# Four graph layers in a four-stage pipeline: layer 0 moved from the first stage to the second

## The chip, the cores and the metric

The kernel runs on one core of one Trainium2 chip. The metric is the device time of one execution in microseconds; the median of three runs before the change is 5727.59 us (5719.75 to 5731.36).

## What is computed

64 graphs, each with 256 nodes, 128 features a node and a symmetric 0/1 adjacency matrix, go through four graph layers. Each layer's result is added to its input and normalised over the features. Shortened:

```python
x: (64, 256, 128) f32, adj: (64, 256, 256) f32 of zeros and ones

# layer 0: maximum over neighbours
p = x @ (W1 - W2);  q = x @ W2
h = relu(p[:, :, None] + q[:, None] + b) * adj[..., None]
x = layernorm(x + max(h, axis=2))
# layer 1: two aggregations and an own term
in_rep, out_rep, node_rep = elu(x @ W.T + b) for three W, b
x = layernorm(x + tanh(concat(adj @ in_rep, node_rep, adj.T @ out_rep) @ W_upd.T + b_upd))
# layer 2: two normalised graph convolutions
x = layernorm(x + norm_A @ (elu(norm_A @ (elu(elu(x @ W0 + b0)) @ W1) + b1) @ W2) + b2)
# layer 3: a message for each edge, normalised, through gelu, summed over neighbours
msg = gelu(layernorm(m_j[:, None] + m_i[:, :, None] + b1))
x = layernorm(x + layernorm(concat(x, sum_j msg * adj) @ W2 + b2))
```

Layers 0 and 3 are the heavy ones: they have a vector of 128 features for each pair of nodes. About one pair in eight is an edge.

## The kernel before

**The sparse layout.** For each graph the nodes are sorted by degree, and the neighbours of all nodes are listed in slots: a node with many neighbours fills many slots. The slots of one half of the nodes lie in `WIDTH` = 4800 columns, and `hot` is a one-hot matrix in fp8 that says, for each column, which node is the neighbour. A matmul of features with `hot` thus gathers the neighbours' features: L665 does it for layer 0, with q split into three bf16 parts, and L728 for layer 3. Layer 0 goes over the 4800 columns of each half in ten tiles of up to 512. In each, three matmuls (L665) write a `bigp` buffer in PSUM, small matmuls (L681) with `lack` and `lack_t` push unfilled slots to a very low value, and `fold` (L492) takes the maximum into `lanes`. After ten tiles the result is transposed (L691), put back in the nodes' order by a matmul with `permT` (L699), added to x and normalised into x1 (L705 to L711). Layer 3 goes over the same columns in tiles of 1024, TODO = 10 of them: `sums_of` makes `pre` (L728, L732), its squares and their sums (L736, L743), and sends the variances through DRAM to get a scale for each column; `last` multiplies (L839), applies Gelu (L841) and folds the sums (L492).

**The stages.** Four generator functions hold the work of one graph. `first` loads the graph, makes the transposed adjacency `aT` (L516, L519), counts and ranks degrees with Sign (L528 to L551), makes the permutation `perm` (L556, L560) and its transpose `permT` (L566 to L581), ranks the neighbours (L585 to L591), writes `hot` (L629, L635), and then does layer 0 (from the projections of L647 to x1). `second` is layer 1 (L215 to L259). `third` is layer 2 (L261 to L317), the projections of layer 3 (L793 to L815) and the first four tiles of `sums_of`. `last` is the other six tiles, Gelu and the sums, and the update with the output.

**The order.** `steps` walks over 64 graphs. In one tick, `last` of graph g, `third` of g+1, `second` of g+2 and `first` of g+3 are recorded together. Each `yield` ends a piece of a stage. `together` takes the pieces in turn: it always calls the generator whose number of calls, divided by its weight, is lowest. The weights are written by hand:

```python
STAGES = [(last, 34), (third, 34), (second, 14), (first, 44)]
e = min(gens, key=lambda e: e[0] / e[1])
```

In this kernel they are the numbers of calls that each stage takes: 34, 34, 14 and 44. The recorded order is the priority order of a scheduler, which may put an instruction that it takes to be ready ahead of one that isn't. After that each engine runs its instructions in a fixed order.

**Buffers.** Pool `state` has two buffers for each name, `hold` has four (`permT`, `lack`, `hot`), `pair` and `work` have one. PSUM is parted in two: four `mm` buffers for all small products (`psum()`), and four `bigp` buffers that layer 0 and layer 3 share. All loads and stores are issued by SP.

Of the kernel before, what the change touches and what calls it, by code (L numbers as in the profile page):

```python
# [10 lines left out]
BF16 = mybir.dt.bfloat16  # L11
# [32 lines left out]
def kernel(  # L44
# [12 lines left out]
    H = N // P  # L57
# [64 lines left out]
    with tc.tile_pool(name="prep", bufs=1) as prep, tc.tile_pool(  # L122
        name="ps_prep", bufs=2, space=bass.MemoryType.PSUM
# [33 lines left out]
    class Shared:  # L157
# [5 lines left out]
        def psum(self):  # L163
            return self.ps_mm.tile([P, 512], F32, name="mm")
# [189 lines left out]
    def sparse(ctx):  # L354
# [24 lines left out]
        g_s0, g_n, g_w = RECTS[-1]  # L379

        ROWS = SLOTS + 2
# [68 lines left out]
        state = ctx.enter_context(tc.tile_pool(name="state", bufs=2))  # L450
        hold = ctx.enter_context(tc.tile_pool(name="hold", bufs=4))
        pair = ctx.enter_context(tc.tile_pool(name="pair", bufs=1))
        work = ctx.enter_context(tc.tile_pool(name="work", bufs=1))
        big = ctx.enter_context(tc.tile_pool(name="big", bufs=2))
        sh = Shared(work, state, ps_mm)
# [13 lines left out]
        def widen(ap, n):  # L469

            return ap.unsqueeze(1).broadcast_to([ap.shape[0], n, ap.shape[1]])
# [30 lines left out]
        def first(g, s):  # L502

            xn = sh.node_tile("x0")
            nc.sync.dma_start(xn, x[ds(g, 1)].rearrange("b (h p) d -> p (b h) d", p=P))
            an = state.tile([P, H, N], F32, name="an")
# [5 lines left out]
            aT = state.tile([P, H, N], F32, name="aT", bufs=3)  # L512
# [6 lines left out]
                nc.scalar.copy(aT[:, hj], pt[:, :N])  # L519
            nzT = as_bf16(aT)  # L520
            yield
            xT = sh.to_features(xn, "xT_0", 1)


            pd = psum()
# [31 lines left out]
            perm = state.tile([P, H, H, N], F32, name="perm", bufs=3)  # L557
# [14 lines left out]
            permT = hold.tile([P, H, H, N], F32, name="permT")  # L572
# [17 lines left out]
            lack = hold.tile([ROWS, H, N], BF16, name="lack")  # L590
# [15 lines left out]
                fl[:, 5:9].rearrange("p (a b) -> p a b", a=H), fv, -1.0, least, ALU.mult, ALU.add  # L606
            )
            nc.vector.tensor_max(viol, viol, fl)
            lack_t = pair.tile([ROWS, H, g_n, g_w], BF16, name="lack_t")
            for h in range(H):  # L610
                nc.vector.tensor_mul(lack_t[:, h], tail, widen(lack[:, h, :g_w], g_n))
            s.update(an=an, aT=aT, perm=perm, permT=permT, lack=lack)

            full = pair.tile([ROWS, H, N], BF16, name="full")
            nc.vector.tensor_scalar(full, lack, 0.0, None, ALU.is_equal)
# [9 lines left out]
            hot = hold.tile([P, H, WIDTH], FP8, name="hot")  # L625
# [8 lines left out]
            for h in range(H):  # L634
# [4 lines left out]
                    ALU.is_equal,  # L639
                    saturate=False,  # L640
                )
            yield
            s["hot"] = hot

            pq = psum()
            for h in range(H):
                nc.tensor.matmul(  # L647
# [129 lines left out]

        def second(g, s):

            yield from sh.layer_1(s, s["an"], s["aT"], s["x1"])  # L780

        def third(g, s):
# [94 lines left out]

        U = next(u for u in (UNROLL, 8, 4, 2, 1) if B % u == 0)
        STAGES = [(last, 34), (third, 34), (second, 14), (first, 44)]

        def steps(g0):
# [215 lines left out]
    with tc.tile_pool(name="flag", bufs=1) as fp, tc.tile_pool(  # L1097
        name="ps_flag", bufs=1, space=bass.MemoryType.PSUM
# [44 lines left out]
```

## Time and profile before

| | us |
|---|---|
| median of three runs | 5727.59 |
| the profiled execution | 5731.62 |
| its span | 5729.7 |
| PE, PEld busy | 4529.9, 2508.7 |
| DVE busy | 4834.4 |
| ACT busy | 4275.2 |
| ACT table loads of L841, L74, L194 | 686.4, 570.9, 283.5 |
| DMA, mean | 64 GB/s |
| granted TensorE clock, mean | 0.862 |

The span runs from the first to the last instruction. PE is the matmul engine, PEld its loading of weights, DVE the vector engine, ACT the scalar engine. By the chain that ended last, PE has 52% of the span, DVE 29%, ACT 11%, DMA 3%. The profile shows the same pattern for each graph from about the fourth on; it is best read one graph at a time.

### The profile page before, as it was taken

What the parts mean: (1) busy time and instruction counts of PE and PEld (TensorE: products, weight loads), DVE (VectorE), ACT (ScalarE), POOL (GpSimd) and SP (SyncE); (2) the same over time, 40 slices, a digit from 0 to 9 for tenths busy, and PEclk for the clock granted to TensorE, in tenths of its full rate; (3) what the DMA queues carried; (4) which work ended last, traced back from release to release, by engine and by line L of the source; (5) the groups of instructions that cost most, each with busy time, mean ns of one, the idle gap of its engine ahead of it and who ended that gap; (6) DMA issues with size and microseconds to landing.
All of it is one profiled execution on the core that took longest, in us unless ns stands there. A gap on an engine that the chain in (4) does not pass through costs nothing.

```text
span 5729.7 us, 83531 instructions
## 1 busy us (share of the span) xinstructions
PE 4529.9 (79%) x27408; PEld 2508.7 (44%) x27408; DVE 4834.4 (84%) x14654; ACT 4275.2 (75%) x6485; POOL 1.9 (0%) x10
## 2 busy tenths in 40 slices
PE   5878878878778778788788788787887887877875
PEld 2444444444444444444444444444444444444443
DVE  6788888888888888888888888888888888888876
ACT  2577777777777777777777777777777777777785
POOL 0000000000000000000000000000000000000000
PEclk8888889889889889888898898898888887888986
DMA  0122222222212221221221222122212212221222
GB/s 22 44 70 63 62 63 72 62 63 66 69 57 70 65 63 63 72 63 62 63 72 62 63 65 70 59 68 65 63 62 72 64 62 63 69 66 60 68 65 74
DMA packets 292813, 365.15 MB, mean 64 GB/s; under 512 B 151952, under 2 KB 210448, under 8 KB 292368
## 3 DMA queue, kind: packets, MB, share of 16 engines
q1 hardware_dynamic: 292368, 359.73, 20.0%
q8 instruction: 217, 3.56, 0.3%
q14 instruction: 228, 1.87, 0.1%
HBM read 345.07 MB, written 14.53 MB: 63 GB/s over the span
## 4 chain that ended last, share of the span: by engine, by line
PE 52%; DVE 29%; ACT 11%; issue 4%; DMA 3%; SPq 0%; DVEq 0%; POOL 0%; ACTq 0%
PE bigp L665 11%; PE bigp L728 8%; DVE pre L839 6%; PE mm L860 5%; DVE lanes L492 4%; PE mm L743 4%; DVE hot L629 4%; DVE pre L732 4%; DVE sums L492 3%; PE bigp L681 3%; DMA rs_s<-scale_line 2%; PE mm L870 2%; PE mm L296 2%; PE mm L699 2%; PE mm L647 2%
## 5 line engine op out<-in xcount | busy, mean ns | idle before, releaser
L665 PE MATMUL bigp<-hot,q 128*128 128x512 fp8e4 (+1 forms) x3840 | 1052.3, 371 | 66.6 <-DVE lanes L492 52.6
L728 PE MATMUL bigp<-hot,c 128*128 128x512 fp8e4 (+1 forms) x3840 | 928.8, 372 | 140.2 <-DVE pre L732 140.2
L732 DVE TENSOR_TENSOR pre<-bigp,dT 128x512 f32<-128x512 f32 (+6 forms) x1664 | 846.3, 530 | 37.8 <-PE bigp L728 33.5
L492 DVE TENSOR_TENSOR lanes<-bigp,lanes 128x512 f32<-128x512 f32 (+6 forms) x1536 | 772.7, 503 | 94.6 <-PE bigp L681 86.9
L839 DVE TENSOR_TENSOR pre<-pre,rs_s 128x1024 f32<-128x1024 f32 (+1 forms) x640 | 732.9, 1150 | 48.6 <-DMA rs_s<-scale_line 48.0
L736 ACT ACTIVATE sq<-pre 128x1024 f32<-128x1024 f32 (+1 forms) x640 | 638.5, 998 | 169.9 <-DVE pre L732 163.9
L841 ACT ACT_TABLE_LOAD x535 | 686.4, 1283 | 9.5
L492 DVE TENSOR_TENSOR sums<-pre,sums 128x1024 f32<-128x1024 f32 (+6 forms) x1024 | 628.8, 614 | 41.2 <-ACT pre L841 40.7
L745 ACT ACTIVATE row<-mm,eps_t 128x256 f32<-128x256 f32 (+1 forms) x640 | 289.6, 453 | 476.9 <-PE mm L743 476.7
L841 ACT ACTIVATE pre<-pre,be,g 128x1024 f32<-128x1024 f32 (+1 forms) x512 | 594.2, 1172 | 57.8 <-DVE pre L839 53.0
L743 PE MATMUL mm<-sq,ones 128*32 128x256 f32 (+1 forms) x5120 | 482.9, 440 | 135.2 <-ACT sq L736 135.2
L74 ACT ACT_TABLE_LOAD x445 | 570.9, 1283 | 7.5
L728 PEld LDWEIGHTS <-c 128*128 128x128 bf16 x3840 | 331.2, 98 | 550.5 <-issue 136.1
L665 PEld LDWEIGHTS <-q 128*128 128x128 bf16 x3840 | 310.8, 97 | 392.6 <-issue 112.0
L296 PE MATMUL mm<-aT,hs 128*128 128x256 f32 x512 | 232.3, 600 | 316.1 <-DVE hs L293 214.8
L629 DVE TENSOR_SCALAR hot<-rank 128x512 fp8e4<-128x512 bf16 (+5 forms) x1536 | 440.5, 348 | 0.0
L681 PEld LDWEIGHTS <-pick 42*128 42x128 bf16 x2944 | 155.8, 95 | 481.5 <-issue 474.2
L296 PEld LDWEIGHTS mm<-aT,hs 128*128 128x128 f32 x512 | 135.6, 293 | 425.8 <-issue 316.1
L860 PE MATMUL mm<-w3u,sums 128*128 128x128 f32 x2048 | 296.7, 289 | 18.4 <-DVE sums L492 16.1
L194 ACT ACT_TABLE_LOAD x221 | 283.5, 1283 | 3.9
L681 PE MATMUL bigp<-lack,pick 42*128 42x36 bf16 (+16 forms) x2944 | 285.7, 187 | 0.0
L860 PEld LDWEIGHTS mm<-w3u,sums 128*128 128x128 f32 x2048 | 254.5, 195 | 37.3 <-issue 17.6
(226 smaller groups left out, 7132.6 us busy)
## 6 DMA issues: line engine op xcount, KB each, us to landing
rs_s<-scale_line SPq DMA_DIRECT2D x512, 512.0 KB
rs_s<-scale_line SPq DMA_DIRECT2D x128, 352.0 KB
an<-in_adj SPq DMA_DIRECT2D x64, 256.0 KB
x<-in_x SPq DMA_DIRECT2D x64, 128.0 KB
line<-row SPq DMA_DIRECT2D x512, 4.0 KB
out<-o SPq DMA_DIRECT2D x64, 128.0 KB
fu<-fulls SPq DMA_DIRECT2D x192, 4.0 KB
vr<-line SPq DMA_DIRECT2D x192, 8.0 KB
```

The lines of the kernel that those rows point to most:

```text
L74: nc.scalar.activation(t, t, AF.Sqrt)
L492: nc.vector.tensor_tensor(lanes[:, :k, :w], src[:, i:i + k], lanes[:, :k, :w], op)
L629: nc.vector.tensor_scalar(hot[:, :, at:at + w], rank[:, :, :w], s0 + i + 1.0 - FAR, None, ALU.is_equal, saturate=False)
L665: nc.tensor.matmul(pt[:, :tl], q3[:, i, h], hot[:, h, t0:t0 + tl], start=i == 0, stop=False)
L681: nc.tensor.matmul(o_, l_, r_, start=False, stop=i == len(todo) - 1)
L728: nc.tensor.matmul(pt[:, :bl], c3[:, k, h], hot[:, h, t0 + b:t0 + b + bl], start=k == 0, stop=k == 2)
L732: nc.vector.tensor_add(block(pre[:, b:], n, w, at), block(pt, n, w, at), widen(dT[:, h, :w], n))
L736: nc.scalar.activation(sq[:, :tl], pre[:, :tl], AF.Square)
L743: nc.tensor.matmul(pr[q * Q:(q + 1) * Q, :tl // 4], ones[:, :Q], v4[:, :, q], start=True, stop=True)
L839: nc.vector.tensor_mul(pre[:, :tl], pre[:, :tl], rs[:, :tl])
L841: nc.scalar.activation(msg[:, :tl], pre[:, :tl], AF.Gelu, bias=be3, scale=g3)
L860: nc.tensor.matmul(pt[:, cols], lanes[:, k, cols], w3u[:, 1], start=k == 0, stop=False)
```

## The change

Layer 0 becomes a function of its own, `layer_0`, which `second` runs ahead of layer 1. With it goes the transpose of the node features, `xT_0`, which stood near the head of `first`. What layer 0 needs of `first` is handed on in `s`: `xn`, `hot`, `lack`, `lack_t` and `permT`. `lack_t` moves from the pool with one buffer to the one with two. The yield at the end of `hot` goes, one is put behind the transposes, and one between layer 0 and layer 1. The weights in `STAGES` stay as they are. The number of calls of `first` becomes 17, that of `second` 42.

```diff
@@ first
             yield
-            xT = sh.to_features(xn, "xT_0", 1)
 
             pd = psum()
...
-            lack_t = pair.tile([ROWS, H, g_n, g_w], BF16, name="lack_t")
+            lack_t = state.tile([ROWS, H, g_n, g_w], BF16, name="lack_t")
             for h in range(H):
                 nc.vector.tensor_mul(lack_t[:, h], tail, widen(lack[:, h, :g_w], g_n))
-            s.update(an=an, aT=aT, perm=perm, permT=permT, lack=lack)
+            s.update(xn=xn, an=an, aT=aT, perm=perm, permT=permT, lack=lack, lack_t=lack_t)
...
                     saturate=False,
                 )
-            yield
             s["hot"] = hot
 
+        def layer_0(s):
+
+            xn, hot, lack, lack_t, permT = (s[n] for n in ("xn", "hot", "lack", "lack_t", "permT"))
+            xT = sh.to_features(xn, "xT_0", 1)
+            yield
             pq = psum()
             for h in range(H):
...
@@ second
         def second(g, s):
 
+            yield from layer_0(s)
+            yield
             yield from sh.layer_1(s, s["an"], s["aT"], s["x1"])
```

More of the change, by code (lines that the diff above doesn't have):

```diff
@@ L641, in first @@
                 )
+            s["hot"] = hot
+        def layer_0(s):
+            xn, hot, lack, lack_t, permT = (s[n] for n in ("xn", "hot", "lack", "lack_t", "permT"))
+            xT = sh.to_features(xn, "xT_0", 1)
             yield
-            s["hot"] = hot
             pq = psum()
```

## The prediction

> **What bounds the kernel now.** Line numbers are those of the kernel before throughout. First the page: how full the engines are, and which waits the costly groups have.
>
> ```profile
> span 5729.7 us, 83531 instructions
> PE 4529.9 (79%) x27408; PEld 2508.7 (44%) x27408; DVE 4834.4 (84%) x14654; ACT 4275.2 (75%) x6485; POOL 1.9 (0%) x10
> L665 PE MATMUL bigp<-hot,q 128*128 128x512 fp8e4 (+1 forms) x3840 | 1052.3, 371 | 66.6 <-DVE lanes L492 52.6
> L629 DVE TENSOR_SCALAR hot<-rank 128x512 fp8e4<-128x512 bf16 (+5 forms) x1536 | 440.5, 348 | 0.0
> ```
>
> No engine is full; three lie between 75 and 84%, so the time is set by how the work of the four stages is laid side by side. The output transfers give the beat: the first is issued at 292.27, the 60th at 5441.70, so one graph takes (5441.70 - 292.27) / 59 = 87.28 us. Next, the busy time in the stretches of one such beat (columns: us, then PE, PEld, DVE, ACT, POOL busy, granted clock, DMA share, GB/s):
>
> ```profile
> 2566.00:2596.00 30.00, 18.64 (x99) 10.82 (x100) 22.84 (x73) 26.02 (x44) 0.00 (x0) 0.66 0.15 45
> 2596.00:2647.00 51.00, 49.04 (x324) 26.93 (x324) 46.52 (x140) 34.98 (x52) 0.00 (x0) 1.00 0.25 79
> 2566.00:2652.50 86.50, 70.57 (x433) 38.87 (x434) 74.86 (x229) 66.43 (x102) 0.00 (x0) 0.86 0.21 65
> 2652.50:2739.00 86.50, 69.93 (x427) 38.22 (x426) 75.29 (x228) 67.72 (x103) 0.00 (x0) 0.88 0.21 66
> ```
>
> The reader sees two regimes. For 30 us the small chained steps of `first`, layer 1 and layer 2 run, side by side: PE is busy 62%, DVE 76%. Then for 51 us layer 0's loop and the sums run: PE 96%, DVE 91%. One beat holds PE 70.2 and DVE 75.1 us of work. The view of waits says what the thin stretch waits for:
>
> ```profile
> PE mm L566 <- DVE perm L560: 245.5, 64, 5.1
> PE mm L296 <- DVE hs L293: 214.8, 67, 8.7
> DVE io L226 <- PE mm L223: 179.7, 64, 3.1
> PE mm L296 <- DVE vr L769: 101.3, 31, 8.7
> ```
>
> Per graph that is 3.8 us for the permutation, 4.9 for layer 2's first product and 2.8 for layer 1's. Last, single steps of the chain, by the timeline:
>
> ```profile
> 2569.59 0.69 PE L207 MATMUL mm<-ident,x 128*128 128x128 f32 x2
> 2642.37 0.38 PE L691 MATMUL mm<-ident,total_m 128*128 128x128 f32 x2
> 2642.59 1.95 PE L699 MATMUL mm<-mk,permT 128*128 128x128 f32 x16
> 2651.88 0.47 PE L207 MATMUL mm<-ident,x 128*128 128x128 f32 x1 [0.82 <-DVE x L180]
> 2572.30 0.76 DVE L226 TENSOR_TENSOR io<-mm,b_io 128x256 f32<-128x256 f32 x2 [3.11 <-PE mm L223]
> 2603.27 1.03 PE L240 MATMUL mm<-an,io 128*128 128x256 f32 x4
> 2580.82 1.28 ACT L194 ACT_TABLE_LOAD   x1
> ```
>
> Layer 0's tail, from L699's end (2644.54) to the transposes of x1 (2651.88), takes 7.3 us, and PE has 14 matmuls of L728 (3.5 us) to do in it. That is the cover to watch.
>
> **What the Trainium skill says.** "TensorE: Matmul & The Clock Gate" (the table of specifications) has the vector and scalar queues as strict FIFO, and lets the tensor queue only pull weight loads ahead; so an instruction that waits holds all behind it. The trace agrees: L566 waits 245.5 us with L743 and L296 behind it. The same page (Part 1) says that an idle tensor engine falls to half its clock: here 0.66 in the thin stretch, 1.00 in the dense one. "ScalarE: Activation LUTs" (What ACT_TABLE_LOAD costs) gives about 1283 ns for a switch of table; the trace has 1283. "Perfetto Trace Analysis" (Optimization Strategy) advises to interleave regimes with different limits; the change interleaves one pair and parts another.
>
> **The change part by part.** Per graph it moves, all from `first` to `second`: 2 transposes, 2 projections, 60 matmuls of L665 and 46 of L681, the folds, 4 transposes, 8 matmuls of L699 and a layernorm. None is added or dropped, no DMA is moved. Table loads in the built order go from 1301 to 1325 (0.4 a graph, 0.5 us on ACT, which has 20 us to spare a beat): nothing. `lack_t` gets a second buffer, and x0 is held one stage longer; its load for the next graph but one can start when L709 has read it, still a beat ahead: nothing. The chain of a graph keeps four stages.
>
> What counts is the order. `together` calls whichever generator has the lowest ratio of calls to weight. Before, calls and weights agree (34, 34, 14, 44). After, `first` has 17 calls under weight 44, and `second` 42 under 14. When `last` and `third` have made their 34, `second` has made 14; its other 28, half of layer 0 and all of layer 1, come with nobody beside them. The scheduler may still lift later ready work, but the built order of PE shows that it hardly does: L691, L699, L207, L223, L230, L238, L240, L249 stand in a row with no L665, L728 or L860 between. So layer 1 follows x1 at once, and layer 2 (L285) follows x2; before, both ran beside `first`.
>
> (1) The exposed chain S, from the last L691 to the next graph's first L665, each step from the rows of the timeline:
> - L691 to the end of L699: 2.2 (2642.37 to 2644.54).
> - to x1's transposes: 7.3 and 8.3 in two beats; I take 7, DVE having less beside it.
> - L207 to L226: 2.7 (2569.59 to 2572.30).
> - L226 0.7, Exp 0.6, one queued L839 1.2 of which 0.9 is seen, L200 and L201 1.1: 3.3.
> - L238 and L240 take 2.1, but ACT stands with load 1.28, Gelu 1.24, load 1.28, Exp 0.42 and copy 0.56 ahead of L249: 2.9 after L201.
> - L249's matmuls and two transposes: 2.2. L253, Tanh, L256: 1.5.
> - x2's layernorm: in DVE's order `kc` (L542) stands inside it and waits for L534, which waits for the aT copies, which ACT does after Tanh: 0.9 + 1.8; then four signs' worth of ACT, a load of 1.28, Sqrt, L75, L180: 6.5 together.
> - transposes, L285, q3: 3.0.
> Sum 31.3 us. PE work in it: 0.4 + 2.0 + 0.4 + 2.1 + 0.6 + 2.1 + 1.9 + 0.4 + 0.6 + 1.9 + 0.8 + 0.4 + 1.6 + 1.1 = 16.1. DVE work, read off its order: 68 instructions with 24.8 us of durations, less the 0.08 by which neighbours overlap (0.68 long, 0.60 apart), 19.3. So DVE idles 12 us in S alone, as much as it does now in a whole beat (87.3 - 75.1 = 12.2).
>
> (2) The rest M. Left are PE 70.2 - 16.1 = 54.1 and DVE 75.1 - 19.3 = 55.8. Now `first`'s chain (perm, rank, hot) lies beside layer 0 and layer 2, so its waits shrink: a gain. At the shares of the dense stretch M is 54.1 / 0.96 = 56.4 by PE and 55.8 / 0.91 = 61.3 by DVE. The 6.9 us of `hot` (440.5 / 64) need no PE, so DVE runs fuller there than 91%, up to 97%: 57.5. But while they run PE's four `bigp` buffers stand full (about 5 us), and it restarts at the lower clock. I take 60.
>
> Beat: 31.3 + 60 = 91.3, 4.0 more than 87.28. Over 59 beats 236 us. The ends: tick 0 loses layer 0, which ran alone (22 groups of L665 and L681 at 0.95, some 21 us); the tail, 282.2 us from the 60th output to the 64th, should keep its length within 5. Net -22. The profiled execution took 5731.62 around its span of 5729.7, so 5731.6 + 236 - 22 = 5946, and the median of the runs is 4 lower: 5942.
>
> Bounds: S from 27 (tail 5, no ACT hold, kc's wait hidden) to 35 (8.3 in the tail, each hop a little late); M from 57.5 to 63. Beat 84.5 to 98: 5545 to 6340.
>
> **The rivals.**
> - Covered, faster: layer 0's matmuls stand where PE now waits for perm and layer 2, 8.7 us a beat, and hot fills DVE's holes; S comes to 27.5, M to 57.5, the beat to 85.0: 5731 - 135 - 22 = 5574, and with DVE at 91% throughout (82.5) 5430. For it: those two waits are the largest of PE's. Against it: they pass to L207, L249 and L285, which now stand alone. It decides when S is below 28 with M below 59.
> - Heavier: every hop of S costs more than its bare row, and PE at half clock runs the start of M late; S 35, M 61, beat 96: 5731 + 515 - 20 = 6226. For it: the 0.66 clock, and 8.3 in one beat.
> - No change: gains and losses cancel, beat within 0.2 of 87.5: 5720.
> - That the change does nothing, the scheduler restoring the old order, the built order excludes.
>
> **How the numbers follow.** Likeliest, slower by the exposed chain: 0.48, 5942, its own range 5800 to 6080. Heavier 0.24. Covered 0.24. No change 0.04. A measurement of this kernel tells 0.2% (11 us) from no change. Faster 0.24, same 0.04, slower 0.72. The range goes to 5560 and 6300, leaving some 0.1 of each rival beyond.
>
> **What would show it.** Right: a beat near 91; PE waits for L180, L201 and L243 at L207, L238 and L249 of some 12 us a graph, with L566's wait below 1; a thin stretch of about 31 us with DVE near 60%. Wrong: DVE over 88% of the span, or layer 1's instructions found beside L665 in time. If the beat is longer but S is 31, M was mis-sized, and PE's waits for `pre` and `lanes` behind hot (L728, L665) will have grown.

## The result and the profile after

The changed kernel takes 6524.14 us, the median of four runs (6522.33 to 6529.15), beside 5729.48 us for the kernel before. The ratio is 1.139, with a 95% interval of 1.137 to 1.141: 13.9% slower, where 3.7% had been forecast. The profiled execution took 6522.96 us. All line numbers from here on are those of the changed kernel; from layer 0 on they lie some three to five above those of the kernel before (L665 is now L668, L691 is L694, L699 is L702, L728 is L731), and before it some one below (L560 and L566, of the permutation, are now L559 and L565).

The page of the changed kernel: span, busy time, and the group that waits longest.

```profile
span 6521.0 us, 83114 instructions
...
PE 4783.0 (73%) x27408; PEld 2664.2 (41%) x27408; DVE 4923.9 (76%) x14654; ACT 4322.3 (66%) x6509; POOL 1.9 (0%) x10
...
L207 PE MATMUL mm<-ident,x 128*128 128x128 f32 x512 | 185.2, 407 | 637.3 <-DVE x L180 637.3
```

PE runs the same 27408 matmuls, and is busy 253 us longer with them (4783.0 - 4529.9), at a mean granted clock of 0.838 where it was 0.862. It stands for another 538 us more (1738 against 1200). One line, the transposes of a normalised x, waits for 637 us.

The outputs give the beat: the first is issued at 277.21, the 60th at 6178.24, so a graph takes 5901.03 / 59 = 100.02 us, 12.74 more than before. The whole difference of the spans then adds up: 59 × 12.74 = 751.6, the head 15.1 shorter, the tail from the 60th output on 54.8 longer (342.8 against 288.0), together 791.3.

The stretches of one beat of the changed kernel, cut where layer 0 ends and where the next layer 0 begins (columns: us, then PE, PEld, DVE, ACT, POOL busy, granted clock, DMA share, GB/s):

```profile
2466.20:2500.10 33.90, 17.19 (x79) 11.88 (x78) 20.22 (x60) 24.80 (x43) 0.00 (x0) 0.69 0.15 48
2500.10:2565.19 65.09, 56.06 (x351) 28.80 (x350) 56.19 (x168) 43.07 (x60) 0.00 (x0) 0.92 0.20 62
2466.20:2565.19 98.99, 73.26 (x429) 40.68 (x428) 76.41 (x228) 67.87 (x103) 0.00 (x0) 0.84 0.18 57
```

The first line is the chain S of the prediction, the second its rest M. In S both PE (51%) and DVE (60%) are half idle. M is no longer like the dense stretch of before either: PE and DVE are busy 86% each, not 96 and 91%. Over 20 beats S is 34.3 us (32.7 to 35.5) and M 65.7.

What PE waits for in the changed kernel, from the view of waits (us in total, times, longest):

```profile
PE mm L207 <- DVE x L180: 637.3, 192, 10.7
PE mm L238 <- DVE io L201: 200.2, 64, 4.5
PE bigp L731 <- DVE pre L735: 177.3, 158, 2.8
...
PE mm L702 <- ACT mk L695: 79.6, 61, 1.4
...
PE mm L249 <- ACT ag L243: 43.2, 64, 0.7
...
PE mm L296 <- DVE hs L293: 12.5, 6, 3.3
...
PE mm L565 <- DVE perm L559: 5.7, 6, 4.6
```

The wait for the permutation has gone from 245.5 us to 5.7, and that of layer 2's product (L296) from 214.8 and 101.3 to 12.5. In their place stand L207, L238, L249 and L702, the steps of layer 0's tail and of layer 1, with next to nothing beside them. The waits of L207, L238 and L249 together are 13.8 us a graph ((637.3 + 200.2 + 43.2) / 64); some 12 had been named as the sign of this cause. PE's own timeline shows them one after the other (start, us, then what it is; in brackets the idle time before it and what ended that):

```profile
2468.86 1.16 PE L702 MATMUL mm<-mk,permT 128*128 128x128 f32 x8 [1.38 <-ACT mk L695]
2475.93 0.73 PE L207 MATMUL mm<-ident,x 128*128 128x128 f32 x2 [5.91 <-DVE x L180]
2477.12 2.07 PE L223 MATMUL mm<-w_ioT,xT 128*128 128x256 f32 x4 [0.46 <-ACT xT L209]
2482.91 2.04 PE L238 MATMUL mm<-aT,io 128*128 128x256 f32 x4 [2.86 <-DVE io L201]
2484.75 1.64 PE L240 MATMUL mm<-an,io 128*128 128x256 f32 x4
2487.07 0.49 PE L249 MATMUL mm<-w_updT,ag 128*128 128x128 f32 x2 [0.68 <-ACT ag L243]
...
2497.09 0.45 PE L207 MATMUL mm<-ident,x 128*128 128x128 f32 x1 [3.16 <-DVE x L180]
```

The order is the one that the prediction read off the built kernel: x1's transposes, layer 1, x2's transposes, each behind a wait. L240, which took 1.03 us where it stood in the dense stretch of before, takes 1.64 here.

### The profile page after: what moved, and what is told of

It reads as the page before. It is cut to its first block, busy times and chain, and to the rows that moved or that the text cites. A ratio compares the mean times of both kernels' runs of the same rounds, so it can differ in the third digit from the quotient of the medians.

```text
span 6521.0 us, 83114 instructions
## 1 busy us (share of the span) xinstructions
PE 4783.0 (73%) x27408; PEld 2664.2 (41%) x27408; DVE 4923.9 (76%) x14654; ACT 4322.3 (66%) x6509; POOL 1.9 (0%) x10
## 4 chain that ended last, share of the span: by engine, by line
PE 39%; DVE 30%; ACT 18%; DMA 9%; issue 4%; SPq 0%; DVEq 0%; ACTq 0%; POOL 0%
DVE pre L735 6%; PE bigp L731 5%; DVE hot L628 5%; DMA rs_s<-scale_line 5%; DVE lanes L492 4%; ACT L74 4%; PE mm L865 4%; PE mm L746 3%; PE bigp L668 3%; PE mm L815 3%; ACT pre L846 3%; ACT L846 3%; DVE sums L492 2%; DMA an<-in_adj 2%; PE mm L802 2%
## 5 line engine op out<-in xcount | busy, mean ns | idle before, releaser
L731 PE MATMUL bigp<-hot,c 128*128 128x512 fp8e4 (+1 forms) x3840 | 991.7, 378 | 211.4 <-DVE pre L735 177.3
L668 PE MATMUL bigp<-hot,q 128*128 128x512 fp8e4 (+1 forms) x3840 | 1045.7, 373 | 126.1 <-DVE lanes L492 71.5
L207 PE MATMUL mm<-ident,x 128*128 128x128 f32 x512 | 185.2, 407 | 637.3 <-DVE x L180 637.3
L492 DVE TENSOR_TENSOR sums<-pre,sums 128x1024 f32<-128x1024 f32 (+6 forms) x1024 | 628.5, 614 | 15.1 <-ACT pre L846 13.5
L748 ACT ACTIVATE row<-mm,eps_t 128x256 f32<-128x256 f32 (+1 forms) x640 | 289.4, 452 | 398.9 <-PE mm L746 398.2
L746 PE MATMUL mm<-sq,ones 128*32 128x256 f32 (+1 forms) x5120 | 460.4, 407 | 106.6 <-ACT sq L739 106.6
L731 PEld LDWEIGHTS <-c 128*128 128x128 bf16 x3840 | 345.9, 100 | 463.9 <-issue 179.7
L668 PEld LDWEIGHTS <-q 128*128 128x128 bf16 x3840 | 327.4, 98 | 426.5 <-issue 122.8
L207 PEld LDWEIGHTS mm<-ident,x 128*128 128x128 f32 x512 | 91.8, 180 | 724.7 <-DVE x L180 476.6
L865 PE MATMUL mm<-w3u,sums 128*128 128x128 f32 x2048 | 296.3, 289 | 16.1 <-DVE sums L492 16.1
L870 ACT COPY ak<-mm 128x256 f32<-128x256 f32 x128 | 46.4, 363 | 383.0 <-PE mm L867 383.0
```

The source lines that it names most:

```text
L492: nc.vector.tensor_tensor(lanes[:, :k, :w], src[:, i:i + k], lanes[:, :k, :w], op)
L668: nc.tensor.matmul(pt[:, :tl], q3[:, i, h], hot[:, h, t0:t0 + tl], start=i == 0, stop=False)
L731: nc.tensor.matmul(pt[:, :bl], c3[:, k, h], hot[:, h, t0 + b:t0 + b + bl], start=k == 0, stop=k == 2)
L746: nc.tensor.matmul(pr[q * Q:(q + 1) * Q, :tl // 4], ones[:, :Q], v4[:, :, q], start=True, stop=True)
L865: nc.tensor.matmul(pt[:, cols], lanes[:, k, cols], w3u[:, 1], start=k == 0, stop=False)
```

## The experiments

Three theories stood at the start. Order: the weights 14 and 44 no longer fit, so that `together` leaves 28 of `second`'s 42 calls alone and the chain is exposed. Chain: with layer 0 ahead of layer 1 in one stage, a graph's layers follow each other in consecutive ticks without slack, and the time is lost whatever the weights. Buffers: `an` has two buffers and is now read last, by L240, near the end of a tick, so that the load of the next adjacency comes late. That wait is new; from the view of waits of the changed kernel:

```profile
DVE nz L509 <- DMA an<-in_adj: 137.7, 61, 3.7
```

Before it was 3.6 us.

**Both weights.** Edit of the changed kernel:

```diff
-        STAGES = [(last, 34), (third, 34), (second, 14), (first, 44)]
+        STAGES = [(last, 34), (third, 34), (second, 42), (first, 17)]
```

> The changed kernel with the weights set to the calls that the stages now take: second 42, first 17. In the built order layer 1's products now stand among L731, L865 and L875. Order theory (the time went because 28 calls of second come alone): most of the loss goes, 5650 to 5900 us, and PE's wait for L180 at L207 falls from 637 us to below 250. Chain theory (layer 0, 1 and 2 of one graph follow each other without slack, whatever the order): 6250 to 6550. Buffer theory (the late load of an, 138 us of direct waits): 6350 to 6550.

Measured: 5882.24 us, 1.026 [1.024, 1.028] of the kernel before. 642 of the 795 us come back with two numbers in a list, and no layer moved. The waits of the chain are gone, from 637.3 us at L207 and 200.2 at L238:

```profile
PE mm L207 <- DVE x L180: 12.2, 20, 3.6
...
PE mm L238 <- DVE io L201: 2.8, 2, 1.9
```

So most of the loss is the order.

**The release of `an`.** The adjacency is symmetric, so L240 can read the same values from `aT`, which leaves `an` free from early in the tick:

```diff
-                nc.tensor.matmul(pg[:, N:], io[:, h, P:], an[:, h], start=h == 0, stop=h == H - 1)
+                nc.tensor.matmul(pg[:, N:], io[:, h, P:], aT[:, h], start=h == 0, stop=h == H - 1)
```

> The changed kernel with L240 reading aT in place of an (the adjacency is symmetric, so the values are the same). Nothing of second reads an any more, so its buffer comes free a tick earlier and the load is early. Buffer theory: the 138 us of DVE waiting at L509 go, with what queues behind them 150 to 300 us: 6220 to 6370. Order theory: the wait stood inside the exposed chain, so between 70 and 140 us go: 6380 to 6455. Chain theory: the same as order theory.

Measured: 6486.91 us, 1.131 [1.130, 1.133]. 37 us come back of a wait that was 138 us in all, less than any of the theories had. Most of the wait had been covered by other waits.

**Both edits together:** the weights 42 and 17, and L240 reading `aT`.

> Both edits: weights 42 and 17, and L240 reading aT. Order theory: no more than 60 us better than the weights alone, since with them L240 comes early in the tick. Buffer theory: the two edits each give what they give alone. If order and buffer are all of it, the time is at or below the kernel before: 5600 to 5750.

Measured: 5589.41 us, 0.975 [0.974, 0.977]. With those weights the edit of L240 brings 293 us, eight times what it brings alone, where the order theory allowed 60. Its direct wait can't be the reason: in the run with both weights alone L509 waited 4.8 us in all. Runs further down bear on what it was.

**The same fault made in the kernel before.** If the order is the cause, layer 0 can be exposed without being moved: with a low weight of `first` its calls come last, behind all others.

```diff
-        STAGES = [(last, 34), (third, 34), (second, 14), (first, 44)]
+        STAGES = [(last, 34), (third, 34), (second, 14), (first, 15)]
```

> The kernel before (layer 0 in first) with first's weight 15 in place of 44, so that some 29 of its 44 calls, layer 0 nearly whole, come with nobody beside them, while layer 1 and layer 2 still lie beside the head of first in the next tick. Order theory: being recorded alone costs by itself, 6000 to 6500. Chain theory: no graph's chain gets tighter by this, at most 2% slower, 5730 to 5850.

Measured: 7143.68 us, 1.247 [1.245, 1.249], 1412 us more than the kernel before and above the range of the order theory. Its page:

```profile
PE 5157.0 (72%) x27408; PEld 2929.9 (41%) x27408; DVE 5000.1 (70%) x14654; ACT 4107.3 (58%) x6325; POOL 1.9 (0%) x10
```

No layer is moved here, and the loss is larger than that of the change. PE is busy 627 us longer with the same matmuls, at a clock of 0.792.

**Each weight alone,** in the changed kernel: `second` 42 with `first` 44, and `first` 17 with `second` 14.

```diff
+        STAGES = [(last, 34), (third, 34), (second, 42), (first, 44)]
```

> One half of the weights: second 42, first left at 44, so the tail of second is covered and the pieces of first still come in the first 40% of the tick. If the exposed chain S (layer 0's tail and layer 1 with nobody beside them) is the loss: 5800 to 6000, near the 5882 of both weights. If the crowding of hot at the head of the stretch M is the loss: 6250 to 6500.

Measured: 6084.55 us, 1.061 [1.058, 1.065]. 440 of the 795 us come back; the time lies between the two ranges.

```diff
+        STAGES = [(last, 34), (third, 34), (second, 14), (first, 17)]
```

> The other half: first 17, second left at 14. The chain S stays alone (the built order shows L702, L207, L223, L230, L238, L249 in a row), hot is spread over the tick. If S is the loss: 6350 to 6550. If the crowding in M is the loss: 5900 to 6150.

Measured: 6495.55 us, 1.133 [1.131, 1.136]. 29 us come back, as the first range had it. Alone the two weights give some 470 us, so some 170 of the 642 come only with both. The stretches show why `first` alone gives little; here S of one beat of this run:

```profile
2462.32:2496.99 34.67, 17.97 (x88) 11.95 (x87) 19.80 (x51) 19.02 (x33) 0.00 (x0) 0.70 0.11 35
```

S is as long as before the edit (34.9 over 20 beats, which are 99.5 long), since `second` still has its 28 calls left. This kernel also spreads `hot` over the tick, and M stays at 64.6 us.

**The edit of L240 in the kernel before:**

> The kernel before with L240 reading aT in place of an, layer 0 in first. If an's buffer binds only because layer 0 moved (L240 comes later in the tick, so the next an but one is late): within 0.5% of before, 5700 to 5760. If freeing an is a gain in any kernel, as large as the 293 us between the runs with the right weights: 5430 to 5520.

Measured: 5833.65 us, 1.019 [1.016, 1.022]. There `an` was free in time (3.6 us of waits), and the edit costs 100 us, which neither range had. The wait for this buffer can't explain it. What the traces show is that the edit changes the order of the other instructions too: ACT's table loads go from 1236 to 1208 here, and from 1274 to 1152 between the runs with 42 and 17. What makes the scheduler come to another order is not shown.

**A higher weight of `second`.** If exposure of the chain is what counts, `second` should end before its neighbours, not with them. With 50, 17 and L240 on `aT`; then the same with L240 on `an`, as in the changed kernel; then with 60, 17 and L240 on `aT`:

```diff
+        STAGES = [(last, 34), (third, 34), (second, 50), (first, 17)]
```

> Weights second 50 and first 17, L240 reading aT: second ends before last and third, so layer 1 and x2's layernorm have their matmuls beside them to the end. If what is left of S costs still: 5450 to 5570, below the 5589 of second 42. If S is covered already at 42: 5570 to 5650.

> Weights second 50 and first 17 on the changed kernel, L240 reading an as it does there. If what the freed an gave at weights 42 and 17 (293 us) is a gain of the buffer: 5500 to 5600. If it came from another interleaving that the edit happened to draw from the scheduler (the direct wait for an was 4.8 us there): within 1.5% of the 5270 with an freed, 5190 to 5350.

```diff
+        STAGES = [(last, 34), (third, 34), (second, 60), (first, 17)]
```

> Weights second 60 and first 17, L240 reading aT: second ends still earlier in the tick. If earlier is better as long as it lies beside last and third: 5150 to 5260. If 50 covers layer 1 fully: 5260 to 5400.

Measured: 5269.97 us (0.920 [0.918, 0.922]) with 50 and `aT`, 5232.25 us (0.913 [0.912, 0.915]) with 50 and `an`, and 5747.22 us (1.003 [1.002, 1.005]) with 60. So layer 0 in the second stage gives the best kernel of this study, 8.7% below the one before, once the weights follow: the chain theory falls. So does the buffer theory: with 50 the edit of L240 costs 38 us. It brought 293 with 42, and cost 100 in the kernel before; the sign turns with the order that comes out. With 60 the chain's waits are back (L207 waits 431.7 us, L238 318.7). Only the run with 50 and `an` fell into a range given for it; 50 with `aT` is below both of its ranges, and 60 above both.

Why 50 beats 42 is not shown. The waits of the chain were gone with 42 already, and with 50 L207 waits longer again, 177.6 us in all against 12.2. What falls between these two kernels (both with `an`) is the idle time of DVE, from some 1060 to 454 us; of that its wait for L731 falls from 370.2 to 53.7.

How the best kernel differs: 80 us of it in four slices (columns as above). No slice has PE below 72% or DVE below 87%.

```profile
2400.00:2420.00 20.00, 18.88 (x123) 8.57 (x123) 18.19 (x44) 19.20 (x30) 0.00 (x0) 1.00 0.27 83
2420.00:2440.00 20.00, 14.51 (x100) 7.90 (x98) 19.69 (x68) 15.96 (x23) 0.00 (x0) 0.84 0.21 72
2440.00:2460.00 20.00, 15.14 (x65) 10.59 (x66) 18.95 (x48) 17.42 (x21) 0.00 (x0) 0.73 0.22 62
2460.00:2480.00 20.00, 17.21 (x134) 10.30 (x132) 17.46 (x71) 12.79 (x27) 0.00 (x0) 1.00 0.22 66
```

Its timeline on PE shows layer 1 with layer 3's matmuls between its steps:

```profile
2456.10 1.03 PE L238 MATMUL mm<-aT,io 128*128 128x256 f32 x4
2456.96 1.03 PE L240 MATMUL mm<-an,io 128*128 128x256 f32 x4
2457.83 3.40 PE L731 MATMUL bigp<-hot,c 128*128 128x512 fp8e4 x15
2461.16 0.64 PE L746 MATMUL mm<-sq,ones 128*32 128x256 f32 x8
2461.73 0.49 PE L249 MATMUL mm<-w_updT,ag 128*128 128x128 f32 x2
```

L249 follows L240 with 4 us of other work in between, where it waited before, and L238 and L240 take 2.06 us together, not 3.68.

**PSUM behind `hot`.** In the changed kernel, one buffer moved from the small products to the shared ones:

```diff
-        ps_mm = ctx.enter_context(tc.tile_pool(name="ps_mm", bufs=4, space=bass.MemoryType.PSUM))
-        ps_big = ctx.enter_context(tc.tile_pool(name="ps_big", bufs=4, space=bass.MemoryType.PSUM))
+        ps_mm = ctx.enter_context(tc.tile_pool(name="ps_mm", bufs=3, space=bass.MemoryType.PSUM))
+        ps_big = ctx.enter_context(tc.tile_pool(name="ps_big", bufs=5, space=bass.MemoryType.PSUM))
```

> The changed kernel with its weights as they are (14 and 44), five bigp buffers and three mm buffers in PSUM in place of four and four. If what made M longer than foreseen is PE standing before full bigp buffers while DVE writes hot (3.8 us of stalls a graph in the trace): 6280 to 6420. If it is the chain of layer 2 and layer 3's projections and the lower clock: 6470 to 6620.

Measured: 6659.16 us, 1.163 [1.161, 1.165]. The time is above both ranges; S rises to 36.0 and M to 66.4. A fifth shared buffer does not shorten M; but the small products lost a buffer to pay for it, and a small gain could be hidden under that loss.

**The kernel before with its long stage ending earlier:**

```diff
+        STAGES = [(last, 34), (third, 34), (second, 14), (first, 52)]
```

> The kernel before with first's weight 52 in place of 44, so that layer 0 ends before last and third do. If ending the chained stage early helps whatever stage it is: 5450 to 5650. If the gain of 50 belongs to layer 0 beside the chain of first: 5680 to 5850.

Measured: 5521.78 us, 0.964 [0.963, 0.966]. As the first range had it, the kernel before also gains, 3.6%, when the stage with the long chain ends ahead of the others; it stays 5.5% above the best one.

**The clock or the chain.** S and M both came out longer than forecast. To tell a lower clock from longer waits, the changed kernel was given matmuls whose result nobody reads, placed so that PE has something to do while the chain waits. The first has 34 a graph (12 behind L702, 12 behind L230, 10 behind L249):

```diff
+        def warm(self, t, n):
+
+            t = t.bitcast(BF16).rearrange("p (n two) -> p n two", two=2)[..., 1]
+            pt = self.psum()
+            for i in range(n):
+                nc.tensor.matmul(pt[:, :t.shape[-1]], t[:, :P], t, start=True, stop=True)
...
+            sh.warm(mk.rearrange("p a b c -> p (a b c)"), 12)
...
+            self.warm(xT, 12)
...
+            self.warm(ag.rearrange("p a b -> p (a b)"), 10)
```

The second has 14 more behind L533, in the last microseconds of S:

```diff
+            pw = psum()
+            for i in range(14):
+                nc.tensor.matmul(pw[:, :N], many_b, nzT[:, 0], start=True, stop=True)
```

> The changed kernel with 34 matmuls a graph added whose result nobody reads (bf16, 12 of 512 columns behind L702 on mk, 12 of 256 behind L230 on xT, 10 of 512 behind L249 on ag), standing in the waits of the thin stretch S in PE's order; all else keeps its order. Clock theory (the excess of S and M over the forecast comes from matmuls at the lower granted clock): S's clock rises from 0.69 to near 1; L223 falls from 2.07 to about 1.03, L238 and L240 together from 3.7 to 2.06, so S falls by 3 to 4 us to about 31 and the beat from 100.0 to 96 or 97: about 6280 to 6330. Latency theory (the chain waits for DVE, ACT and semaphores, and the clock is a by-product): the beat stays at 100 within 0.5: 6490 to 6560. Crowding: if the added matmuls push the chain's own back, the beat is above 100.5.

> As e13_warm, and 14 more such matmuls (256 columns, on the transposed adjacency of first) behind L533, so that PE is also busy in the last 3 us of S, just ahead of layer 0's loop. Clock theory: M, too, starts at the full clock, and its PE work falls from 56 towards 54: beat 95 to 96, some 40 to 100 us below e13_warm. If M's excess of 5.7 us is the chain of layers 2 and 3 and the waits behind hot, M stays at 65 to 66 and the time is that of e13_warm within 30 us.

Measured: 6627.32 us (1.159 [1.156, 1.162]) with 34, 6214.44 us (1.086 [1.084, 1.088]) with 48. The first fits none of its expectations as a whole: over 20 beats S fell to 30.7 us, as the clock theory has it, and M rose to 71.1. ACT has 6267 instructions instead of 6509 there (242 table loads fewer), PE waits 173.1 us for `hs` where it waited 12.5, and 232.5 for `sq` where it waited 106.6: it runs in another order, and its total says nothing on the clock. The second kept 6509; it has the beat of its clock theory and the M of the other. One beat of it, cut as above:

```profile
2447.42:2476.89 29.47, 21.25 (x125) 13.93 (x126) 20.17 (x60) 23.70 (x43) 0.00 (x0) 0.94 0.17 55
2476.89:2541.20 64.31, 55.70 (x344) 28.90 (x344) 54.80 (x162) 42.65 (x60) 0.00 (x0) 0.92 0.20 63
```

S has 60 DVE and 43 ACT instructions in both kernels, with busy times within 1.1 us, PE does 4 us more, and S is 4.4 us shorter, at a clock of 0.94 instead of 0.69. Its layer 1 with the matmuls that nobody reads between, on PE (in this kernel L208 is the added matmul, L246 and L248 are the former L238 and L240):

```profile
2460.93 1.62 PE L208 MATMUL mm<-xT 128*128 128x256 bf16 x12
2464.08 1.10 PE L246 MATMUL mm<-aT,io 128*128 128x256 f32 x4 [1.53 <-DVE io L201]
2465.02 1.03 PE L248 MATMUL mm<-an,io 128*128 128x256 f32 x4
2466.86 0.49 PE L257 MATMUL mm<-w_updT,ag 128*128 128x128 f32 x2 [0.82 <-ACT ag L251]
```

Over the beats S is 29.8 us, M 65.4, the beat 95.2 between the outputs: 59 × (100.02 - 95.19) = 285 of the 307 us between the two spans.

The 4.5 us by which S falls are not the clock alone, for in x2's layernorm ACT runs in another order. In the changed kernel a `row` (L748), which waits for PE, and a sign stand ahead of the table load for the square root. With the 48 matmuls the load and the root come first, and the `row` (there L761) after them. ACT in the changed kernel, then with the 48:

```profile
2493.99 0.41 ACT L748 ACTIVATE row<-mm,eps_t 128x176 f32<-128x176 f32 x1 [1.61 <-PE mm L746]
...
2494.87 1.28 ACT L74 ACT_TABLE_LOAD   x1
```

```profile
2472.00 1.28 ACT L74 ACT_TABLE_LOAD   x1
...
2474.97 0.41 ACT L761 ACTIVATE row<-mm,eps_t 128x176 f32<-128x176 f32 x1 [0.42 <-PE mm L759]
```

Over the 20 beats the step from x2's sum (L256) to its last normalised half (L180) falls from 5.64 to 3.21 us, 2.4 of the 4.5; what the order and what the clock did there was not separated. Of the 2.1 us that fall elsewhere, 1.3 lie between L201 and the copy `ag`, where L238 and L240 run, and fit the clock.

M has hardly moved. In its first 4 us the clock was 0.63 and is now 1.00, in the beats shown; the ten us from 27 us on, with layer 3's projections, have 0.66 in both. The changed kernel, then that with the 48 (columns as above):

```profile
2500.10:2504.10 4.00, 4.00 (x21) 1.99 (x19) 3.49 (x12) 1.25 (x3) 0.00 (x0) 0.63 0.00 0
2527.00:2537.00 10.00, 7.80 (x39) 5.44 (x32) 7.11 (x24) 6.89 (x10) 0.00 (x0) 0.66 0.33 108
```

```profile
2476.89:2480.89 4.00, 3.98 (x33) 1.94 (x33) 3.68 (x15) 3.18 (x6) 0.00 (x0) 1.00 0.00 0
2503.80:2513.80 10.00, 7.56 (x25) 5.45 (x26) 6.66 (x22) 5.80 (x10) 0.00 (x0) 0.66 0.32 107
```

So M's excess is not the low clock at its start. The low clock in its middle was not lifted by any run.

## Why the prediction was wrong in size and right in kind

The reason given was right. S exists, with PE and DVE half idle; the thin stretch has DVE at 60%, as forecast; the waits stand at L207, L238 and L249, and L565's is gone; DVE falls to 76% of the span. That exposure, and not the longer chain or a buffer, is the cause of most of the loss was shown by the weights: 642 us given back in the changed kernel, with the waits of the chain gone, and a larger loss made in the kernel before. The rival of cover fell, since next to nothing lay beside S.

The time was missed by 582 us, above the range. The failed step is the sum of (1) and (2), in this order of size:

- **The rest M, 60 us forecast, 65.7 measured: 5.7 × 59 = 336 us.** The shares of the dense stretch of before, PE 96% and DVE 91%, were laid on a stretch that has other contents. In the dense stretch ran layer 0's loop and layer 3's sums, and no chain. In M there also run the chain of `first` up to `hot`, layer 2, and layer 3's projections, so both engines reach 86%. In the dissected beat M is 65.1 us: PE is busy 56.1 of them, where 54.1 had been reckoned (at a mean clock of 0.92, where the dense stretch had 1.00), and stands 9.0, where M = 60 left 5.9. The waits: 3.8 behind `hot`, 1.5 for `sq`, 2.2 in layer 3's projections (x3T, `dn`), the rest for `pre` and `lanes`. The forecast called the shrinking waits of `first` a gain, and did not count that its chain, moved beside layer 0, brings the thin work with it. That it isn't the clock at M's start is shown, and with `hot` spread over the tick (`first` at 17) M is still 64.6; what the clock of 0.66 in M's middle and each of these waits cost was read off the trace and not separated by a run, and stays open.
- **The chain S, 31.3 forecast, 34.3 measured: 3.0 × 59 = 177 us.** Most hops were near: layer 0's tail 5.9 against 7, x2's layernorm 5.7 against 6.5, L201's end 3.5 against 3.3. The matmuls and copies were not. L238 and L240 up to the copy took 4.25 us instead of 2.9, because L240's row came from the dense stretch, where its four matmuls took 1.03 us; here those of L238 take 2.04 and those of L240 1.64. With the clock kept up, in the last experiment, the same hop took 2.87. Up to the end of L702 it took 3.8 instead of 2.2, because ACT's copy `mk` stands behind a Gelu and a load of a table. The prediction had quoted 0.66 for the thin stretch, and yet took L240's duration from a row where the clock was 1.00. The two hops that were forecast too long, by 1.1 and 0.8 us, hid a part of the error.
- **The ends, -22 forecast, +39.7 measured: 62 us.** The head became 15.1 shorter, near the 21 forecast. The tail, said to keep its length within 5, grew by 54.8. The outputs in it come at distances of 99.7, 87.6, 100.6 and 49.1 us, and before of 86.4, 81.9, 64.6 and 49.4: the last graphs, too, seem to wait for the S of a tick in which little else is left. No run tests this by itself; with the weights 50 and 17 the tail is 285.2.

These make 575 of the 577 us between the profiled execution and its forecast, 5946. The rival "heavier" had S near with 35, and fell short for the same M (61). Its S was in part luck: not every hop cost more than its row, two cost less.

One sum of the prediction is off: the PE terms listed under (1) add up to 16.3 us, not 16.1. It changes nothing, since the 60 for M was set by DVE's terms.

A claim of no cost failed as well, though cheaply: that the loads stay a beat ahead. It was made for x0, and `an` was not looked at. L240 now reads `an` in the middle of S (at 2484.75 in the beat shown), its next load is issued at 2486.42, and L509 can start only at 2489.08; it waits for 138 us in all. Freed, it gave back 37.

## What to carry to other kernels

When work moves between stages that are interleaved by weights, count the calls again, and try the stage with the longest chain ending somewhat before its neighbours: here that decided between 13.9% slower and 8.7% faster, while ending it earlier still (60) lost the gain. Busy shares and durations belong to the stretch in which they were measured; a stretch with other contents needs its own sum, and a matmul that comes to stand alone is priced by a row from a thin stretch (L238 took 2.04 us there, 1.03 in the best kernel). A change of order by itself moves this kernel by some hundred us either way, so a difference of that size is not to be put down to a buffer or a wait without a run that takes just that away.

## What the hardware showed

The same 27408 matmuls kept PE busy 4304.1 us in the best kernel (clock 0.920) and 5157.0 in the worst (0.792). "TensorE: Matmul & The Clock Gate" of the Trainium skill (Part 1) says that idle time, of a window of about 3.4 us, throttles the tensor engine, and that sustained work lifts the throttle; the traces agree, with 0.69 in S and 0.92 in M. What had not been expected is that work that nobody reads can pay: with 48 such matmuls a graph the clock rose from 0.838 to 0.922 and the changed kernel came out 310 us faster, 4.7%, though a part of it lies in the step of S where ACT's order changed as well. It isn't a sure gain: with 34 of them the clock rose to 0.871, and in the order that came out the kernel was 103 us slower. The best kernel, which has layer 3's matmuls between the steps of layer 1, is another 982 us below; how much of that is the clock was not separated. "Perfetto Trace Analysis" (Optimization Strategy) advises to interleave regimes with different limits, and the weights of 50 and 17 do so.
